# A selective scan in tiles of 4 states x 32 channels, with B and C as broadcast tables

## The chip, the core and the metric

The kernel runs on one core of a Trainium2 chip. The metric is device time in microseconds of one execution, as the median of several runs. Inside the core five engines run side by side, each taking its own instructions in order: TensorE (PE, matrix products), VectorE (DVE), ScalarE (ACT), GpSimd (POOL), and SyncE (SP), whose queue issues most transfers here. The transfers themselves run on 16 DMA engines.

## The reference

The input x is 32 sequences (a batch index b) of 512 tokens with 256 features. A Mamba block, an MLP and a mixture of experts follow one another. What the change touches is the selective scan over 512 inner channels with 16 states each:

```python
xc = silu(conv(xc) + conv_b)
dbc = xc @ x_proj_w.T
dt, Bm, Cm = split(dbc, [16, 32])
dt = softplus(dt @ dt_proj_w.T + dt_proj_b)
A = -exp(A_log)
def step(h, inp):
    dt_t, B_t, C_t, x_t = inp
    dA = exp(dt_t[..., None] * A)
    h = dA * h + (dt_t * x_t)[..., None] * B_t[:, None, :]
    y = einsum('bdn,bn->bd', h, C_t)
    return h, y
y = ys + xc * D_param
y = y * silu(z)
return y @ out_proj_w.T
```

Before it stands a layer norm and the input projection to xc and z. After it come the residual and a layer norm, an MLP with GELU, another layer norm, a router that picks two of eight experts of width 128 beside a shared expert, and a last layer norm. Everything is float32.

## The kernel before

One sequence is one unit of work, and there are 32. For each, `front` normalizes x, transposes it, projects it, does the convolution on DVE (the line of `pin`, L260), and makes dbc, B, C, dt and dt x (`dtx`). dt and dt x are written to scratch in DRAM (`sdt`, `sdx`). B and C are spread over the partitions by two matmuls with the constant `spread` (L291) and copied by ACT to SBUF (`bcr`, tag `bc0` and `bc1`, L293).

The scan needs every channel once for each of its 16 states. A tile has 128 partitions: 16 states times 8 channels (NS = 16, ND = 8), and 512 time steps on the free axis. The 512 channels are 4 blocks j of 128, each of 4 groups q, each of 4 tiles w. A step k takes two of the w (WS = 2) at once, so there are 32 steps for a sequence and 1024 in all. For each step:

- `load` (L336) reads dt and dt x from the scratch with every row repeated for the 16 states: two transfers of 512 KB on SP's queue, into `dtr` (5 buffers) and `u` (8 buffers). The load is written three steps ahead (N_LOAD).
- `times_b` (L356) multiplies u by B in place, on POOL where q is 0, and on DVE for the other three groups. DVE takes B from a PSUM copy (`brep`, one per sequence, L363).
- ACT makes the decay exp(A dt) of each of the two tiles in PSUM (`pda`, two buffers, L420), and DVE runs the recurrence in place in u (L424).
- POOL multiplies u by C (L426).
- When the four w of a group are done, `summed` (L385) adds over the states: four matmuls with the constant `gather` put the sums in four strips of 32 rows of `py` (L388). Each w has its own strip. `skip` (L383) puts D times xc in first.

At the end of a block j DVE multiplies `py` by the gate (L406), and this is xc for the output projection. Since a tile's rows come out in the order w, q, d, the z half of the input projection and the rows of the output projection are stored in that order by the host code.

Beside the scan of sequence b, a generator `fill` runs the `finish` of b - 1: `middle` (projection, MLP), then `front` of b + 1, then `back` (router and experts). The functions yield between pieces, and the loop at the end deals the pieces out over the scan's steps (N_FRONT and N_FINISH are the counts of pieces). The order of instructions in an engine's queue follows this text only roughly: the framework that places tiles moves instructions by its own estimates of when their inputs are ready, as far as the dependencies allow. `later` holds matmuls back: LAG = 1 entry stays in it.

[...] A transposed activation `hT` (MLP) and `x1T` (experts), and `h` and the experts' sum `acc`, have one buffer each.

## Time and profile before

| | |
|---|---|
| median of 3 runs | 5920.9 us (5915.45 to 5924.98) |
| the profiled execution | 5914.54 us |
| its span, first to last instruction | 5912.8 us |
| mean granted TensorE clock | 0.883 |
| moved by DMA | 1184.34 MB, 200 GB/s |

The costliest groups of instructions. Each line has the source line, engine and operation, what is written and read, the shapes and the count; then the busy time, the mean of one in ns, and the idle time of the engine just before it with what ended most of it:

```profile
L426 POOL TENSOR_TENSOR u<-u,bc 128x1024 f32<-128x1024 f32 x1024 | 2411.3, 2358 | 1637.3 <-DVE u L424 961.5
L424 DVE TENSOR_TENSOR_SCAN u<-pda,u 128x512 f32<-128x512 f32 x2048 | 2448.6, 1208 | 193.8 <-ACT pda L420 119.4
L420 ACT ACTIVATE pda<-dtr,a_neg 128x512 f32<-128x512 f32 x2048 | 1401.7, 689 | 1764.1 <-DVE u L424 1666.6
L388 PE MATMUL py<-u,gather 128*32 128x512 f32 x4096 | 1139.3, 682 | 766.1 <-POOL u L426 565.9
L366 DVE TENSOR_TENSOR u<-u,brep 128x1024 f32<-128x1024 f32 x768 | 918.5, 1202 | 200.3 <-DMA u<-sdx 177.6
...
L366 POOL TENSOR_TENSOR u<-u,bc 128x1024 f32<-128x1024 f32 x256 | 603.2, 2357 | 237.7 <-DMA u<-sdx 227.1
```

And the transfers by issue, with the size and the median time from issue to landing in us:

```profile
dtr<-sdt SPq DMA_DIRECT2D x1024, 512.0 KB, 7.3
u<-sdx SPq DMA_DIRECT2D x1024, 512.0 KB, 8.4
sdt<-dt SPq DMA_DIRECT2D x64, 512.0 KB, 2.8
sdx<-dtx SPq DMA_DIRECT2D x64, 512.0 KB, 3.1
x<-in_x_dram SPq DMA_DIRECT2D x32, 512.0 KB, 4.7
out_dram<-acc SPq DMA_DIRECT2D x32, 512.0 KB, 5.8
```

A float32 matmul is two instructions in the profile, so 4096 gather instructions are 2048 matmuls. Busy time of an engine is a sum over the whole span; idle time matters only on an engine that sets the end.

### The profile page before, as it was taken

What the parts mean: (1) busy time and instruction counts of PE and PEld (TensorE: products, weight loads), DVE (VectorE), ACT (ScalarE), POOL (GpSimd) and SP (SyncE); (2) the same over time, 40 slices, a digit from 0 to 9 for tenths busy, and PEclk for the clock granted to TensorE, in tenths of its full rate; (3) what the DMA queues carried; (4) which work ended last, traced back from release to release, by engine and by line L of the source; (5) the groups of instructions that cost most, each with busy time, mean ns of one, the idle gap of its engine ahead of it and who ended that gap; (6) DMA issues with size and microseconds to landing.
All of it is one profiled execution on the core that took longest, in us unless ns stands there. A gap on an engine that the chain in (4) does not pass through costs nothing.

```text
span 5912.8 us, 51778 instructions
## 1 busy us (share of the span) xinstructions
PE 4769.0 (81%) x14464; PEld 2025.0 (34%) x14464; DVE 4936.8 (83%) x7308; ACT 2817.1 (48%) x4224; POOL 3654.8 (62%) x2128
## 2 busy tenths in 40 slices
PE   6688778888788887788887888878888878888787
PEld 1133333333333333333333333333333333333343
DVE  5788888888888888888888888888888888888885
ACT  4445554445544445544455444455444554444542
POOL 3766666656666666666566566666666665666652
PEclk7688889988898898899888898988999888989898
DMA  7978888787887878887878878887878788788871
GB/s 193 239 195 200 211 202 206 201 205 203 207 210 199 210 193 210 199 208 197 209 199 209 203 196 212 201 212 202 206 195 211 194 214 203 198 209 200 210 188 52
DMA packets 367215, 1184.34 MB, mean 200 GB/s; under 512 B 36928, under 2 KB 70848, under 8 KB 366800
## 3 DMA queue, kind: packets, MB, share of 16 engines
q1 hardware_dynamic: 363936, 1175.65, 79.6%
q10 hardware_dynamic: 2992, 5.38, 0.3%
q8 instruction: 117, 1.92, 0.1%
q14 instruction: 170, 1.39, 0.1%
HBM read 1097.00 MB, written 83.89 MB: 200 GB/s over the span
## 4 chain that ended last, share of the span: by engine, by line
PE 29%; DVE 27%; DMA 16%; POOL 14%; issue 8%; ACT 3%; SPq 0%; POOLq 0%; DVEq 0%; ACTq 0%
DMA u<-sdx 16%; DVE u L424 13%; PE py L388 8%; POOL u L426 7%; POOL u L366 4%; DVE acc L574 3%; PE pd L212 3%; PE po L212 3%; DVE u L366 3%; PE pm L205 3%; PE pu L205 2%; PE pdbc L278 2%; PE pg L205 2%; POOL dt L317 2%; DVE the L598 1%
## 5 line engine op out<-in xcount | busy, mean ns | idle before, releaser
L426 POOL TENSOR_TENSOR u<-u,bc 128x1024 f32<-128x1024 f32 x1024 | 2411.3, 2358 | 1637.3 <-DVE u L424 961.5
L424 DVE TENSOR_TENSOR_SCAN u<-pda,u 128x512 f32<-128x512 f32 x2048 | 2448.6, 1208 | 193.8 <-ACT pda L420 119.4
L420 ACT ACTIVATE pda<-dtr,a_neg 128x512 f32<-128x512 f32 x2048 | 1401.7, 689 | 1764.1 <-DVE u L424 1666.6
L388 PE MATMUL py<-u,gather 128*32 128x512 f32 x4096 | 1139.3, 682 | 766.1 <-POOL u L426 565.9
L366 DVE TENSOR_TENSOR u<-u,brep 128x1024 f32<-128x1024 f32 x768 | 918.5, 1202 | 200.3 <-DMA u<-sdx 177.6
L366 POOL TENSOR_TENSOR u<-u,bc 128x1024 f32<-128x1024 f32 x256 | 603.2, 2357 | 237.7 <-DMA u<-sdx 227.1
L205 PE MATMUL pg<-x1T,wg_sb 128*128 128x512 f32 x1152 | 633.0, 656 | 99.1 <-DVE the L598 99.0
L212 PE MATMUL pd<-wd_sb,he 128*128 128x256 f32 x2304 | 647.5, 395 | 43.2 <-DVE acc L574 37.7
L388 PEld LDWEIGHTS py<-u,gather 128*32 128x32 f32 x4096 | 156.4, 114 | 1406.4 <-POOL u L426 880.8
L212 PEld LDWEIGHTS pd<-wd_sb,he 128*128 128x128 f32 x2304 | 410.7, 190 | 501.6 <-DVE acc L574 232.3
L205 PE MATMUL pu<-x1T,wu_sb 128*128 128x512 f32 x1152 | 581.5, 620 | 0.0
L574 DVE SCALAR_TENSOR_TENSOR acc<-pd,cwt,acc 128x256 f32<-128x256 f32 x1024 | 445.8, 470 | 44.6 <-PE pd L212 44.4
L205 PE MATMUL pin<-xnT,in_sb 128*128 128x512 f32 x512 | 310.2, 740 | 81.4 <-DVE xc L272 80.0
L205 PEld LDWEIGHTS pg<-x1T,wg_sb 128*128 128x128 f32 x1152 | 220.5, 205 | 301.8 <-DVE the L598 146.4
L205 PEld LDWEIGHTS pu<-x1T,wu_sb 128*128 128x128 f32 x1152 | 230.6, 200 | 259.5 <-issue 242.4
L260 DVE SCALAR_TENSOR_TENSOR pin<-xpad,half,pin 128x512 f32<-128x512 f32 x384 | 275.0, 744 | 40.9 <-issue 17.1
L205 PE MATMUL pm<-hT,w_sb 128*128 128x512 f32 x512 | 270.2, 676 | 23.2 <-ACT hT L458 23.2
L591 ACT ACTIVATE the<-pg 128x512 f32<-128x512 f32 x288 | 170.3, 591 | 225.3 <-PE pg L205 224.9
L205 PE MATMUL pz<-xnT,in_sb 128*128 128x512 f32 x512 | 263.7, 600 | 0.3 <-DVE the L598 0.3
L212 PE MATMUL po<-out_sb,xc 128*128 128x256 f32 x1024 | 246.9, 394 | 1.6 <-DVE xc L406 1.6
L212 PE MATMUL pm<-w_sb,hid 128*128 128x256 f32 x1024 | 226.2, 379 | 0.0
L212 PEld LDWEIGHTS po<-out_sb,xc 128*128 128x128 f32 x1024 | 194.3, 195 | 89.5 <-DVE u L424 52.0
(112 smaller groups left out, 4911.0 us busy)
## 6 DMA issues: line engine op xcount, KB each, us to landing
dtr<-sdt SPq DMA_DIRECT2D x1024, 512.0 KB, 7.3
u<-sdx SPq DMA_DIRECT2D x1024, 512.0 KB, 8.4
sdt<-dt SPq DMA_DIRECT2D x64, 512.0 KB, 2.8
sdx<-dtx SPq DMA_DIRECT2D x64, 512.0 KB, 3.1
x<-in_x_dram SPq DMA_DIRECT2D x32, 512.0 KB, 4.7
out_dram<-acc SPq DMA_DIRECT2D x32, 512.0 KB, 5.8
wg_sb<-in_w_g_dram ACTq DMA_DIRECT2D x1, 1152.0 KB, 11.7
wu_sb<-in_w_u_dram ACTq DMA_DIRECT2D x1, 1152.0 KB, 6.8
```

The lines of the kernel that those rows point to most:

```text
L205: nc.tensor.matmul(p, w[:, k, cols], src[:, k, :], start=(k == 0), stop=(k == KM - 1))
L212: nc.tensor.matmul(p, part[:, c * P : (c + 1) * P], w[:, j, :], start=(j == 0), stop=(j == len(parts) - 1),)
L260: nc.vector.scalar_tensor_tensor(pa, xp[:, i : i + S], half[:, w0 + i : w0 + i + 1], pa, ALU.mult, ALU.add,)
L278: nc.tensor.matmul(pd[: R + 2 * NS, :], xp_sb[:, j, :], xcs[j], start=(j == 0), stop=(j == NJ - 1),)
L317: nc.gpsimd.tensor_tensor(dt[:, js, :], dt[:, js, :], dtx[:, js, :], ALU.add)
L366: eng.tensor_tensor(u, u, rep.unsqueeze(1).to_broadcast([P, WS, S]), ALU.mult)
L388: nc.tensor.matmul(py[w * n : (w + 1) * n, :], gather[:, q, :], u, start=False, stop=(q == NQ - 1),)
L420: nc.scalar.activation(pda, dtr[:, w, :], AF.Exp, scale=a_neg[:, i : i + 1])
L424: nc.vector.tensor_tensor_scan(uw, pda, uw, 0.0, ALU.mult, ALU.add)
L426: nc.gpsimd.tensor_tensor(u, u, bcr[1].unsqueeze(1).to_broadcast([P, WS, S]), ALU.mult)
L574: nc.vector.scalar_tensor_tensor(a, p, cw[:, c, e : e + 1], a, ALU.mult, ALU.add)
L591: nc.scalar.activation(th, pg, AF.Tanh, scale=0.5)
```

## The change

A tile now holds 4 states of 32 channels (NP = 4, ND = 32), with the 512 time steps as before. A block j of 128 channels is 4 groups c of 32, and the 16 states are 4 groups of 4, taken two at a time (GS = 2), so a step is (b, j, c, g) with g 0 or 1, and there are again 32 steps of two tiles for a sequence.

- `load` brings dt and dt x of a group c once, as tiles of 256 KB (`dtr`, `dxr`, three buffers each), with each row repeated for 4 states. Both steps of the group, four tiles, use them. The load is written two groups ahead.
- B and C differ over the states of a tile, and no longer only by partition copies made on the chip: `front` writes the 32 rows of B and C to scratch (`rows`), and `table` reads them back, repeated over the 32 channels, as four tables of 512 KB for a sequence (two halves g of each; three buffers for B and three for C). The spread matmuls and their copies go.
- `times_b` multiplies dt x by B into a new tile u. Where DVE does it (c from 1 to 3), dt x is first copied by ACT to the PSUM bank that `brep` had (`dx`, one buffer), once for each group c.
- `summed` has one 128 x 32 `gather`; it runs for a pair of groups c - 1 and c at the same g, so its four matmuls go to two strips of `py`, each twice. `later` counts in steps, LAG = 2.
- A block's rows are now in natural order, and the host code no longer permutes the projections.
- `acc` is `h` itself, and `hT` and `x1T` share a buffer (`mT`). `front` has one piece fewer.

```diff
@@ -26,16 +26,19 @@
 EPS = 1e-5
 
 
-ND = P // NS
-W = 4
-NQ = P // (W * ND)
+
+NP = 4
+NG = NS // NP
+ND = P // NP
+NC4 = P // ND
+GS = 2
 
 
...
@@ -116,32 +119,13 @@
 
 
 
-
-    spread = const.tile([R + 2 * NS, 2, P], F32, name="spread")
-    for a in range(2):
-        n0 = R + a * NS
-        nc.vector.tensor_copy(
-            spread[:, a, :].rearrange("p (n d) -> p n d", d=ND),
-            ident[: R + 2 * NS, n0 : n0 + NS].unsqueeze(2).to_broadcast(
-                [R + 2 * NS, NS, ND]
-            ),
-        )
-    gather = const.tile([P, NQ, NQ * ND], F32, name="gather")
-    nc.gpsimd.memset(gather, 0.0)
-    for q in range(NQ):
-        nc.vector.tensor_reduce(
-            gather[:, q, q * ND : (q + 1) * ND],
-            ident.rearrange("p (n d) -> p d n", d=ND),
-            AX.X,
-            ALU.add,
-        )
+    gather = const.tile([P, ND], F32, name="gather")
+    nc.vector.tensor_reduce(
+        gather, ident.rearrange("p (d n) -> p d n", n=NP), AX.X, ALU.add
+    )
     skip = const.tile([P, NJ, P], F32, name="skip")
     for j in range(NJ):
-        nc.vector.tensor_scalar_mul(
-            skip[:, j, :].rearrange("p (w q d) -> p w q d", w=W, q=NQ),
-            ident.rearrange("p (q d w) -> p w q d", w=W, q=NQ),
-            col("dp", j),
-        )
+        nc.vector.tensor_scalar_mul(skip[:, j, :], ident, col("dp", j))
 
     out_sb = const.tile([P, NJ, DM], F32, name="out_sb")
     w1_sb = const.tile([P, KM, 2 * DM], F32, name="w1_sb")
...
@@ -285,14 +269,8 @@
         yield
         dbc = work.tile([R + 2 * NS, S], F32, tag="dbc", name=f"dbc_{b}", bufs=1)
         nc.scalar.copy(dbc, pd[: R + 2 * NS, :])
-        bcr = []
-        for a in range(2):
-            pb = ps.tile([P, S], F32, tag="tk", name=f"pbc_{b}_{a}")
-            nc.tensor.matmul(pb, spread[:, a, :], dbc, start=True, stop=True)
-            t = work.tile([P, S], F32, tag=f"bc{a}", name=f"bc{a}_{b}")
-            nc.scalar.copy(t, pb)
-            bcr.append(t)
-        yield
+        rows = scr.tile([2, NS, S], F32, tag="rows", name=f"rows_{b}")
+        nc.sync.dma_start(rows.rearrange("a n t -> (a n) t"), dbc[R : R + 2 * NS, :])
 
 
         dt = work.tile([P, NJ, S], F32, tag="dt", name=f"dt_{b}", bufs=1)
...
-
-
-
+        got[b] = (xt, xnT, xcs, rows, sdt, sdx)
+
+
+
+
+    NH = NG // GS
     steps = [
-        (b, j, q, w)
+        (b, j, c, g)
         for b in range(NB)
         for j in range(NJ)
-        for q in range(NQ)
-        for w in range(0, W, WS)
+        for c in range(NC4)
+        for g in range(NH)
     ]
-    dtrs, us, breps = {}, {}, {}
+    per = NJ * NC4 * NH
+    dtrs, dxrs, dxps, us, bcs = {}, {}, {}, {}, {}
 
     def load(k):
-        b, j, q, w = steps[k]
+
+        b, j, c, _ = steps[k]
         _, _, _, _, sdt, sdx = fronts[b]
-        for tag, src, into, bufs in (
-            ("dtr", sdt, dtrs, DT_BUFS),
-            ("u", sdx, us, U_BUFS),
-        ):
-            t = work.tile([P, WS, S], F32, tag=tag, name=f"{tag}_{b}_{j}_{q}_{w}", bufs=bufs)
-            rows = src[j, q * W * ND : (q + 1) * W * ND, :]
+        for tag, src, into in (("dtr", sdt, dtrs), ("dxr", sdx, dxrs)):
+            t = work.tile([P, S], F32, tag=tag, name=f"{tag}_{b}_{j}_{c}", bufs=DT_BUFS)
             nc.sync.dma_start(
-                t.rearrange("p w t -> p (w t)"),
-                rows.rearrange("(d w) t -> d w t", w=W)[:, w : w + WS, :]
+                t,
+                src[j, c * ND : (c + 1) * ND, :].unsqueeze(1).to_broadcast([ND, NP, S]),
+            )
+            into[k // NH] = t
+
+    def table(a, b, g):
+
+        if (a, b, g) not in bcs:
+            t = work.tile([P, GS, S], F32, tag=f"bc{a}", name=f"bc{a}_{b}_{g}", bufs=NH + 1)
+            n0 = g * GS * NP
+            nc.sync.dma_start(
+                t.rearrange("p g t -> p (g t)"),
+                fronts[b][3][a, n0 : n0 + GS * NP, :]
+                .rearrange("(n g) t -> n (g t)", g=GS)
                 .unsqueeze(0)
-                .to_broadcast([NS, ND, WS, S]),
-            )
-            into[k] = t
+                .to_broadcast([ND, NP, GS * S]),
+            )
+            bcs[a, b, g] = t
+        return bcs[a, b, g]
 
     def by_pool(k):
         return steps[k][2] == 0
 
     def times_b(k):
-        b = steps[k][0]
+        b, j, c, g = steps[k]
+        kc = k // NH
         if by_pool(k):
-            eng, rep = nc.gpsimd, fronts[b][3][0]
+            eng, dx = nc.gpsimd, dxrs[kc]
         else:
-            if b not in breps:
-                breps[b] = ps.tile([P, S], F32, tag="brep", name=f"brep_{b}", bufs=1)
-                nc.scalar.copy(breps[b], fronts[b][3][0])
-            eng, rep = nc.vector, breps[b]
-        u = us[k]
-        eng.tensor_tensor(u, u, rep.unsqueeze(1).to_broadcast([P, WS, S]), ALU.mult)
+            if kc not in dxps:
+                dxps[kc] = ps.tile([P, S], F32, tag="dx", name=f"dx_{b}_{j}_{c}", bufs=1)
+                nc.scalar.copy(dxps[kc], dxrs[kc])
+            eng, dx = nc.vector, dxps[kc]
+        u = work.tile([P, GS, S], F32, tag="u", name=f"u_{b}_{j}_{c}_{g}", bufs=U_BUFS)
+        eng.tensor_tensor(
+            u, dx.unsqueeze(1).to_broadcast([P, GS, S]), table(0, b, g), ALU.mult
+        )
+        us[k] = u
 
     def ahead(k):
 
-        if k + N_LOAD < len(steps):
-            load(k + N_LOAD)
+        if k % NH == 0 and k + N_LOAD * NH < len(steps):
+            load(k + N_LOAD * NH)
         if k + 1 < len(steps) and by_pool(k + 1):
             times_b(k + 1)
         if k < len(steps) and not by_pool(k):
             times_b(k)
 
     def scan(b):
-        xt, xnT, ys, bcr, _, _ = fronts[b]
+        xt, xnT, ys, _, _, _ = fronts[b]
+
 
         later = []
 
         def skipped(j, py):
             nc.tensor.matmul(py, skip[:, j, :], ys[j], start=True, stop=False)
 
-        def summed(q, py, tiles):
-            n = NQ * ND
-            for w, u in enumerate(tiles):
-                nc.tensor.matmul(
-                    py[w * n : (w + 1) * n, :],
-                    gather[:, q, :],
-                    u,
-                    start=False,
-                    stop=(q == NQ - 1),
-                )
+        def summed(py, c, g, pair):
+
+            for i in range(GS):
+                for dc, u in enumerate(pair):
+                    r = (c + dc) * ND
+                    nc.tensor.matmul(
+                        py[r : r + ND, :],
+                        gather,
+                        u[:, i, :],
+                        start=False,
+                        stop=(g == NH - 1 and i == GS - 1),
+                    )
 
         def gate(j):
 
...
@@ -405,36 +402,32 @@
         def gated(j, py, th):
             nc.vector.scalar_tensor_tensor(ys[j], py, 0.5, th, ALU.mult, ALU.mult)
 
-        per = len(steps) // NB
-        tiles = []
         for k in range(b * per, (b + 1) * per):
-            _, j, q, w0 = steps[k]
-            u, dtr = us.pop(k), dtrs.pop(k)
-            if q == 0 and w0 == 0:
+            _, j, c, g = steps[k]
+            u, dtr = us[k], dtrs[k // NH]
+            if c == 0 and g == 0:
                 py = ps.tile([P, S], F32, tag="py", name=f"py_{b}_{j}", bufs=1)
-                later.append(partial(skipped, j, py))
+                later.append((k + LAG, partial(skipped, j, py)))
             ahead(k + 1)
-            for w in range(WS):
-                pda = ps.tile([P, S], F32, tag="pda", name=f"pda_{b}_{j}_{q}_{w0 + w}")
-                i = (j * NQ + q) * W + w0 + w
-                nc.scalar.activation(
-                    pda, dtr[:, w, :], AF.Exp, scale=a_neg[:, i : i + 1]
-                )
-                uw = u[:, w, :]
-                nc.vector.tensor_tensor_scan(uw, pda, uw, 0.0, ALU.mult, ALU.add)
-                tiles.append(uw)
-            nc.gpsimd.tensor_tensor(
-                u, u, bcr[1].unsqueeze(1).to_broadcast([P, WS, S]), ALU.mult
-            )
-            if len(tiles) == W:
-                later.append(partial(summed, q, py, tiles))
-                tiles = []
-                if q == NQ - 1:
-                    later.append(partial(gated, j, py, gate(j)))
-                while len(later) > LAG:
-                    later.pop(0)()
-            yield
-        for f in later:
+            if k == (b + 1) * per - 2 * NC4 and b + 1 < NB:
+                table(0, b + 1, 0)
+                table(1, b + 1, 0)
+            for i in range(GS):
+                pda = ps.tile([P, S], F32, tag="pda", name=f"pda_{b}_{j}_{c}_{g}_{i}")
+                a = (j * NC4 + c) * NG + g * GS + i
+                nc.scalar.activation(pda, dtr, AF.Exp, scale=a_neg[:, a : a + 1])
+                ui = u[:, i, :]
+                nc.vector.tensor_tensor_scan(ui, pda, ui, 0.0, ALU.mult, ALU.add)
+            nc.gpsimd.tensor_tensor(u, u, table(1, b, g), ALU.mult)
+            if c % 2 == 1:
+                pair = (us.pop(k - NH), us.pop(k))
+                later.append((k + LAG, partial(summed, py, c - 1, g, pair)))
+                if c == NC4 - 1 and g == NH - 1:
+                    later.append((k + LAG, partial(gated, j, py, gate(j))))
+            while later and later[0][0] <= k:
+                later.pop(0)[1]()
+            yield
+        for _, f in later:
             f()
 
...
@@ -447,7 +440,7 @@
             nc.vector.tensor_tensor(h[:, c, :], xt[:, c, :], po[:, :DM], ALU.add)
         mr, rs = layernorm(h, f"b{b}")
         yield
-        hT = work.tile([P, KM, S], F32, tag="hT", name=f"hT_{b}", bufs=1)
+        hT = work.tile([P, KM, S], F32, tag="mT", name=f"hT_{b}", bufs=1)
 
         def get(c):
...
@@ -533,8 +526,8 @@
     def back(b, h):
         mr, rs = layernorm(h, f"c{b}")
         yield
-        acc = work.tile([P, NC, DM], F32, tag="acc", name=f"acc_{b}", bufs=1)
-        x1T = work.tile([P, KM, S], F32, tag="x1T", name=f"x1T_{b}", bufs=1)
+        acc = h
+        x1T = work.tile([P, KM, S], F32, tag="mT", name=f"x1T_{b}", bufs=1)
 
         def get(c):
             normalize(acc[:, c, :], h[:, c, :], mr, rs, c)
...
     run(front(0, fronts))
     load_late_weights()
-    for k in range(N_LOAD):
-        load(k)
+    for i in range(N_LOAD):
+        load(i * NH)
+    table(1, 0, 0)
     times_b(0)
     ahead(0)
     fill, n_fill = (front(1, fronts), 2 * N_FRONT) if NB > 1 else (iter(()), 0)
     for b in range(NB):
...
 
-LAG = 1
-WS = 2
-N_LOAD = 3
-N_FRONT = 30
-N_FINISH = 88
-DT_BUFS = 5
+LAG = 2
+N_LOAD = 2
+N_FRONT = 29
+N_FINISH = 87
+DT_BUFS = 3
 U_BUFS = 8
...
     def states(v):
 
-        v = v.reshape(NJ, NQ, ND, W, NS)
-        return v.transpose(4, 2, 0, 1, 3).reshape(P, -1)
-
-
-    o = _np.arange(DI).reshape(NJ, NQ, ND, W).transpose(0, 3, 1, 2).reshape(-1)
-    in_w = a["attn_in_proj_w"]
-    in_w = _np.concatenate([in_w[:DI], in_w[DI:][o]], axis=0)
+        v = v.reshape(NJ, NC4, ND, NG // GS, NP, GS)
+        return v.transpose(2, 4, 0, 1, 3, 5).reshape(P, -1)
...
         ("x", a["attn_x"]),
         ("vecs", vecs),
-        ("in_w", in_w.T),
+        ("in_w", a["attn_in_proj_w"].T),
         ("xp_w", a["attn_x_proj_w"].T),
         ("dt_w", a["attn_dt_proj_w"].T),
-        ("out_w", a["attn_out_proj_w"].T[o]),
+        ("out_w", a["attn_out_proj_w"].T),
         ("m_w1", a["attn_mlp_w1"].T),
```

## What the change is predicted to do

> **What bounds the kernel now.** I read the busy shares first, then the slices in time, the chain of waits, the waits of each engine, and last one batch cut into its stages.
>
> ```profile
> PE 4769.0 (81%) x14464; PEld 2025.0 (34%) x14464; DVE 4936.8 (83%) x7308; ACT 2817.1 (48%) x4224; POOL 3654.8 (62%) x2128
> ...
> DMA  7978888787887878887878878887878788788871
> ...
> q1 hardware_dynamic: 363936, 1175.65, 79.6%
> ...
> PE 29%; DVE 27%; DMA 16%; POOL 14%; issue 8%; ACT 3%; SPq 0%; POOLq 0%; DVEq 0%; ACTq 0%
> DMA u<-sdx 16%; DVE u L424 13%; PE py L388 8%; POOL u L426 7%; POOL u L366 4%; DVE acc L574 3%; PE pd L212 3%; PE po L212 3%; DVE u L366 3%; PE pm L205 3%; PE pu L205 2%; PE pdbc L278 2%; PE pg L205 2%; POOL dt L317 2%; DVE the L598 1%
> ```
>
> No engine is full: VectorE (DVE) works 4936.8 of 5912.8 us, so it idles 976, and that is all a change that leaves its work alone can win. The DMA engines are busy to 7 or 8 tenths in every slice, and the largest single piece of the last chain is a transfer, the load of u (16%, some 946 us). What of it costs DVE time is in the waits:
>
> ```profile
> DVE u L366 <- DMA u<-sdx: 177.6, 79, 4.2
> DVE acc L572 <- PE pd L212: 168.0, 62, 6.7
> DVE u L424 <- ACT pda L420: 119.4, 112, 5.1
> DVE h L485 <- PE pm L212: 102.6, 35, 16.8
> ...
> DVE st_a L175 <- DMA x<-in_x_dram: 51.4, 29, 5.4
> DVE acc L574 <- PE pd L212: 44.4, 98, 1.3
> ...
> DVE u L424 <- POOL u L366: 22.0, 7, 5.8
> ...
> POOL u L366 <- DMA u<-sdx: 227.1, 135, 6.9
> POOL u L426 <- DMA u<-sdx: 168.6, 34, 7.1
> ...
> ACT pda L420 <- DMA dtr<-sdt: 87.7, 40, 2.7
> ```
>
> DVE waits directly for DMA (177.6 + 51.4), and behind ACT and GpSimd (POOL) that wait for it. A second family, 315 us (168.0 + 102.6 + 44.4), is DVE waiting for matmuls; TensorE (PE) runs in order, and its gather matmuls wait for POOL. One batch by stages (from 2947 us: MLP, next front's convolution, its dt part, experts):
>
> ```profile
> 2947.00:2985.00 38.00, 28.24 (x90) 13.82 (x89) 28.81 (x44) 21.13 (x31) 27.64 (x19) 0.87 0.81 207
> 2985.00:3030.00 45.00, 30.87 (x88) 8.75 (x89) 39.42 (x50) 22.61 (x37) 28.77 (x20) 0.81 0.93 222
> 3030.00:3060.00 30.00, 26.18 (x63) 9.58 (x62) 22.69 (x31) 20.00 (x29) 18.97 (x9) 0.72 0.63 176
> 3060.00:3130.00 70.00, 64.74 (x217) 30.93 (x216) 63.39 (x107) 24.33 (x39) 38.75 (x20) 1.00 0.79 204
> ```
>
> The columns after the length are busy time of PE, weight loads, DVE, ACT, POOL, then PE's clock, DMA share and GB/s. DVE idles 9.2, 5.6, 7.3 and 6.6 us, 28.7 in 183. In the expert stage PE is 92% busy at full clock: there PE is a second bound.
>
> **What the Trainium skill says.** "Perfetto Trace Analysis", Identifying the Most-Contended Engine: occupancy is a fair measure for the vector engines, matmul busy time is not. So DVE's 83% is read as a floor and PE's 81% is not; the trace agrees, since the same gather group takes 1.05 or 1.92 us with the clock. "DMA: Bandwidth & Descriptors", Specifications: line rate needs pieces of at least 512 B. The new loads have 2 KB rows instead of 4 KB; the trace has 2 KB rows in the writes of dt (512 KB landed in 2.8 us), so I see no penalty beyond a bounded one. "TensorEngine Tiling (Array Packing)", Key Properties: different tiles of the array run in parallel. The trace agrees (the gather of four tiles, eight instructions, takes 1.06 us; that of one, two instructions, 1.05). "GPSIMD Engine Reference", Specifications: its SBUF interface is shared with DVE when DVE has two SBUF inputs. That is avoided before (brep in PSUM) and after (dx in PSUM); DVE's multiplication stays one SBUF and one PSUM input, so I keep its 1202 ns.
>
> **Part by part.**
>
> *Loads.* Gone: 2048 loads of 512 KB (dtr, u), 1073.7 MB. New: 1024 of 256 KB (dtr, dxr), 268.4 MB, 128 tables of 512 KB, 67.1 MB, 32 small writes of rows, 2 MB. Of 1184 MB some 448 are left: DMA share 79.6 x 448 / 1184 = 30% at the same rate, 50% at worst with the smaller rows. Either way the queue is open. Loads are asked for two channel groups ahead (four steps, some 22 us at 5.77 us per step = 5912.8 / 1024), against 7.3 and 8.4 us to landing now. So direct waits go: 177.6 all; of 51.4 for x some 40 (the landing itself stays); of the 119.4 for the exponentials some 60, since ACT's wait for dtr is 87.7; of the 22.0 for POOL's product 20. Together 298. Bounds: 178 (u alone) and 339 (177.6 + 51.4 + 87.7 + 22.0).
>
> *What POOL's lateness costs.* POOL waits 227.1 + 168.6 = 396 us for u. PE waits 566 us for POOL's products, and 200 for a POOL queue held up elsewhere. I give PE's share 396 / 766 = 0.52 of the 315 us that DVE waits for matmuls: 163. Below it is 0, if POOL is then late for another reason; above, 315.
>
> *Multiplication by B.* 768 on DVE at 1202 ns and 256 on POOL at 2357, as before; the output is now a new tile. It needs no transfer into u, so a u buffer is taken at the product, not a DMA earlier. Tiles of a pair wait two steps longer for their gather, and LAG is 2: the eight buffers are held about as long as before without the transfer. Zero.
>
> *Copies of dx.* 12 per batch, 384 x 592 ns (row of brep's copy) = 227 us on ACT, less 64 copies of bc (37.1) and 32 of brep (18.9): +171, ACT goes from 48 to 51%. ACT idles 1667 us waiting for the scan, which hides them. But there is one bank: the copy must wait for DVE's last product with the old dx, and DVE's next product waits for the copy. In the changed program's order two to eight DVE instructions (2.4 us and more) stand between. Only at the batch end do four normalizations, which now wait 3.9 us for POOL's mr_d once a batch, stand between two copies; behind the waiting product on DVE are scans, for which POOL waits. I take 0.1 us a copy: 38. Bounds 0 and 0.8 us a copy (307).
>
> *Gather matmuls.* Still 2048 (4096 instructions), but a group of four now falls on two column strips (c and c+1), each twice in turn. Two can run side by side, where eight instructions of four tiles take 1.06 us now. I went through both instruction orders, counting each unbroken run as 0.85 us per layer and 0.2 for its start: 26.9 us a batch before (the trace has 1139.3 / 32 = 35.6, with cold clocks and broken runs), 36.1 after. So +9.2 us a batch, 2.6 in the expert stage, 6.6 elsewhere. The two spread matmuls save 66.3 in all, not on the path. The 2.6 count in full (PE 92% busy): 83. Of the 6.6 a fifth, PE being 69 to 87% busy there: 42. Together 125. Bounds: 0 and 294.
>
> *Tables.* Four per batch. Those of the second half are asked for when first used, so POOL stands once or twice a batch for a transfer of some 5 us; behind it on POOL are C products, with PE two steps behind. On SP's queue the C table waits for POOL's last use of the old one, with the output write and a load for two groups ahead behind it. I take 1 us a batch on DVE's path: 30; bounds 0 and 100.
>
> *acc in h, hT and x1T in one buffer, LAG, constants.* The next h waits for the output write (5.8 us to landing); the last normalizations stand in ACT's order ahead of exponentials for six scans and a product, over 8 us of DVE work, that come before it. Zero, at most 3 us a batch (93) without that cover.
>
> Sum: 5912.8 - 298 - 163 + 38 + 125 + 30 = 5646 as a span. The profiled run took 5914.5 with 1.7 around its span, and the median of the runs is 6.4 above it, so 5654; I say **5655 us**. DVE would then idle some 710 us instead of 976. What is late next: PE in the expert stage, the normalization chain over POOL and ACT after each batch's scan, and DVE itself.
>
> **Rivals.**
> 1. *DVE's floor comes nearer* (15%). DMA held back more than its own waits show: direct 339, all 163 of POOL's, gather and copies hidden: 5921 - 502 = 5419, reaching up to 5500. For it: 16% of the chain is the u load. Against: the expert stage has few DMA waits and a full PE.
> 2. *PE takes the place of DMA* (18%). All 9.2 us a batch land on the path (294), POOL's part does not return: 5921 - 298 + 294 - 66 = 5851 with the spread matmuls saved; between 5770 and 5909. For it: PE at 92% with experts. Against: in the other three stages PE idles 28 us of 113 (9.8 + 14.1 + 3.8), at clocks of 0.72 to 0.87.
> 3. *The single dx bank makes it slower* (12%). Every change of channel group is a chain DVE, ACT, DVE. With t us of stall on each of 384 copies, gather 125 and tables 30, it loses as soon as 384 t + 155 passes 461, t = 0.8 us. ACT is in order, and an ACT instruction waiting for PE or POOL (225 us for pg, 126 for mr_b) ahead of a copy would give that. At t = 1.5: 5921 + 576 + 155 - 461 = 6191. Against: the slack in the order above.
>
> **How the numbers follow.** Forecast 55% (5500 to 5770), rivals 15, 18 and 12. Measurements tell 0.2% (12 us) from no change. Of the second rival 3 points lie within that, and 1 of the third: same 0.04. Slower 0.11, faster 0.85. The range leaves out about half of rival 1 and most of rival 3: 5440 to 5870.
>
> **What would show it.** DMA share 30 to 50%. The waits of DVE and POOL for u by DMA gone, and no wait for the table or dxr above 60 us in their place. DVE busy within 1% of 4937. Gather busy up by 200 to 350 us. DVE's wait for the dx copy under 60 us; above 300 rival 3 is right. A DVE wait for pd and pm above 350 us with PE over 88% busy means rival 2. The prediction fails if DVE's idle time stays above 900 us or falls below 500.

## The result, and the profile after

| | before | after |
|---|---|---|
| median, 4 runs each on one chip | 5922.9 us | 5846.0 us (5845.5 to 5850.2) |
| ratio, 95% interval | | 0.9873 (0.9856 to 0.9890) |
| span of the profiled run | 5912.8 us | 5843.9 us |
| DVE busy, idle | 4936.8, 976.0 | 4950.2, 893.7 |
| moved by DMA | 1184 MB | 448 MB |

The change makes the kernel faster by 1.3%, 77 us, where 266 were forecast. Of all executions in this document one, of the later run onecopy_fix, took 7420.2 us at a mean granted TensorE clock of 0.602 instead of 0.917, and it is left out of that run's figures.

Busy times, the main DMA queue and the last chain, from the page of after:

```profile
PE 4875.3 (83%) x14336; PEld 2073.3 (35%) x14336; DVE 4950.2 (85%) x7303; ACT 2965.3 (51%) x4512; POOL 3649.2 (62%) x2127
...
q1 hardware_dynamic: 236448, 439.49, 22.6%
...
DVE 42%; PE 36%; POOL 9%; ACT 7%; issue 4%; DMA 0%; ACTq 0%; DVEq 0%; POOLq 0%
DVE u L420 21%; PE py L385 11%; DVE u L357 6%; PE pg L189 6%; PE pd L196 6%; POOL u L421 5%; PE pu L189 4%; DVE pin L244 4%; DVE h L567 2%; PE pm L189 2%; PE pm L196 2%; ACT pda L418 2%; POOL dt L295 2%; PE pz L189 1%; POOL dtx L297 1%
```

DMA is gone from the chain (16% before) and idle for three quarters of the time. Still DVE idles 894 us. What it waits for now, by total us, number of waits and the longest:

```profile
DVE m L501 <- PE pg L543: 198.2, 32, 10.4
DVE u L420 <- ACT pda L418: 117.3, 96, 2.5
DVE xc L403 <- PE py L385: 113.2, 66, 8.6
DVE the L591 <- ACT the L584: 99.9, 68, 2.1
DVE u L357 <- ACT dx L354: 78.1, 31, 2.5
DVE h L478 <- PE pm L196: 74.7, 35, 17.5
DVE h L565 <- PE pd L196: 61.5, 63, 1.3
DVE h L567 <- PE pd L196: 51.3, 100, 0.8
...
DVE st_a L159 <- DMA x<-in_x_dram: 7.8, 3, 5.4
```

The 177.6 us for u are gone, those for x fell from 51.4 to 7.8, and those for pd and pm from 315 to 187.5. Against that, four waits grew by 424 us: the router's maximum for pg from 16.4 to 198.2, the expert's tanh from 12.2 to 99.9, the gate for py from 36.5 to 113.2, and the copy of dx, which is new, 78.1. Only the last belongs to an edit directly. In before these lines read:

```profile
DVE xc L406 <- PE py L388: 36.5, 36, 9.5
...
DVE m L508 <- PE pg L550: 16.4, 3, 10.3
...
DVE the L598 <- ACT the L591: 12.2, 10, 5.6
```

Where the largest arises is seen in the timeline of one batch (start, duration, and in brackets the idle time before with its releaser):

```profile
2983.03 3.63 PE L385 MATMUL py<-u,gather 128*32 128x512 f32 x8 [0.74 <-POOL u L421]
2983.29 1.21 DVE L357 TENSOR_TENSOR u<-dx,bc 128x1024 f32<-128x1024 f32 x1
2983.33 1.91 ACT L291 ACTIVATE dt<-dt 128x2048 f32<-128x2048 f32 x1
2985.14 0.57 ACT L537 COPY x1T<-tp_c 128x512 f32<-128x512 f32 x1
...
2988.63 1.62 PE L543 MATMUL pg<-gt_sb,x1T 128*128 128x8 f32 x14
...
2990.29 0.19 DVE L501 TENSOR_REDUCE m<-pg 128x4 f32<-128x32 f32 x1 [5.79 <-PE pg L543]
```

DVE's reduction L501 stands in its queue ahead of two scans. It waits 5.79 us for router products that stand on PE behind eight gather instructions of 3.63 us, and whose input x1T stands on ACT behind the logarithm of dt. No transfer and no full engine holds this up; it is where the instructions stand. The clock has a part in it: from 2983.00 to 2987.00 us TensorE was granted 0.55 of full speed on the mean, and the eight gather instructions took 3.63 us, where the same eight take 1.91 us at a granted clock of 1.00 (after_sched3, below). They took 3.5 us or more ahead of the router in 30 of the 32 batches, so some 1.7 us of each such wait is put down to the clock here. This is an estimate from these two durations, and no run tests it.

### The profile page after: what moved, and what is told of

Its sections match the earlier page's. It is cut to its first block, busy times and chain, and to the rows that moved or that the text cites. A ratio compares the mean times of both kernels' runs of the same rounds, so it can differ in the third digit from the quotient of the medians.

```text
span 5843.9 us, 47922 instructions
## 1 busy us (share of the span) xinstructions
PE 4875.3 (83%) x14336; PEld 2073.3 (35%) x14336; DVE 4950.2 (85%) x7303; ACT 2965.3 (51%) x4512; POOL 3649.2 (62%) x2127
## 3 DMA queue, kind: packets, MB, share of 16 engines
q1 hardware_dynamic: 236448, 439.49, 22.6%
## 4 chain that ended last, share of the span: by engine, by line
DVE 42%; PE 36%; POOL 9%; ACT 7%; issue 4%; DMA 0%; ACTq 0%; DVEq 0%; POOLq 0%
DVE u L420 21%; PE py L385 11%; DVE u L357 6%; PE pg L189 6%; PE pd L196 6%; POOL u L421 5%; PE pu L189 4%; DVE pin L244 4%; DVE h L567 2%; PE pm L189 2%; PE pm L196 2%; ACT pda L418 2%; POOL dt L295 2%; PE pz L189 1%; POOL dtx L297 1%
## 5 line engine op out<-in xcount | busy, mean ns | idle before, releaser
L421 POOL TENSOR_TENSOR u<-u,bc 128x1024 f32<-128x1024 f32 x1024 | 2410.5, 2356 | 1778.4 <-DVE u L420 1691.1
L420 DVE TENSOR_TENSOR_SCAN u<-pda,u 128x512 f32<-128x512 f32 x2048 | 2439.5, 1211 | 121.4 <-ACT pda L418 117.3
L385 PE MATMUL py<-u,gather 128*32 128x512 f32 x4096 | 1389.1, 664 | 442.0 <-POOL u L421 393.9
L357 DVE TENSOR_TENSOR u<-dx,bc 128x1024 f32<-128x1024 f32 x768 | 923.6, 1210 | 83.2 <-ACT dx L354 78.1
L385 PEld LDWEIGHTS py<-u,gather 128*32 128x32 f32 x4096 | 238.5, 115 | 1249.6 <-POOL u L421 606.5
L357 POOL TENSOR_TENSOR u<-dxr,bc 128x1024 f32<-128x1024 f32 x256 | 602.4, 2353 | 4.8 <-PE py L385 2.8
L196 PEld LDWEIGHTS pd<-wd_sb,he 128*128 128x128 f32 x2304 | 421.0, 189 | 403.9 <-DVE h L567 168.0
L567 DVE SCALAR_TENSOR_TENSOR h<-pd,cwt,h 128x256 f32<-128x256 f32 x1024 | 450.0, 480 | 55.6 <-PE pd L196 51.3
L196 PE MATMUL po<-out_sb,xc 128*128 128x256 f32 x1024 | 303.0, 452 | 53.8 <-DVE h L440 28.6
L189 PE MATMUL pin<-xnT,in_sb 128*128 128x512 f32 x512 | 252.0, 625 | 52.9 <-DVE xc L256 49.8
L262 PE MATMUL pdbc<-xc,xp_sb 128*48 128x512 f32 x256 | 175.0, 846 | 131.9 <-DVE xc L256 131.8
L591 DVE SCALAR_TENSOR_TENSOR the<-the,pg 128x512 f32<-128x512 f32 x288 | 195.8, 680 | 99.9 <-ACT the L584 99.9
L189 PE MATMUL pm<-hT,w_sb 128*128 128x512 f32 x512 | 239.3, 611 | 43.2 <-ACT hT L451 22.6
```

Source lines behind the costliest of these rows:

```text
L189: nc.tensor.matmul(p, w[:, k, cols], src[:, k, :], start=(k == 0), stop=(k == KM - 1))
L196: nc.tensor.matmul(p, part[:, c * P : (c + 1) * P], w[:, j, :], start=(j == 0), stop=(j == len(parts) - 1),)
L262: nc.tensor.matmul(pd[: R + 2 * NS, :], xp_sb[:, j, :], xcs[j], start=(j == 0), stop=(j == NJ - 1),)
L357: eng.tensor_tensor(u, dx.unsqueeze(1).to_broadcast([P, GS, S]), table(0, b, g), ALU.mult)
L385: nc.tensor.matmul(py[r : r + ND, :], gather, u[:, i, :], start=False, stop=(g == NH - 1 and i == GS - 1),)
L420: nc.vector.tensor_tensor_scan(ui, pda, ui, 0.0, ALU.mult, ALU.add)
```

## The experiments

Ratios are to the kernel before on the same chip. The measured medians, with the runs of before from 5911.6 to 5929.6:

| run | us | ratio (95%) |
|---|---|---|
| wide | 5890.2 | 0.9948 (0.9933 to 0.9962) |
| b_narrow | 5835.4 | 0.9858 (0.9841 to 0.9876) |
| b_quarter | 5789.3 | 0.9777 (0.9762 to 0.9791) |
| b_quarter_narrow | 5698.9 | 0.9626 (0.9611 to 0.9640) |
| before_ordn | 5842.0 | 0.9883 (0.9853 to 0.9914) |
| wide_fix | 5796.9 | 0.9812 (0.9783 to 0.9841) |
| onecopy_fix | 5847.1 | 0.9871 (0.9849 to 0.9893) |
| b_quarter_fix | 5910.5 | 1.0001 (0.9988 to 1.0014) |
| b_half_fix | 5752.0 | 0.9710 (0.9691 to 0.9730) |
| after_more | 6734.7 | 1.1376 (1.1347 to 1.1405) |
| after_order | 5808.2 | 0.9832 (0.9798 to 0.9866) |
| after_sched | 5456.8 | 0.9214 (0.9196 to 0.9232) |
| before_sched | 5785.8 | 0.9764 (0.9744 to 0.9783) |
| b_half_sched | 5768.1 | 0.9739 (0.9719 to 0.9759) |
| wide_sched | 5462.7 | 0.9225 (0.9209 to 0.9240) |
| after_sched2 | 5545.1 | 0.9364 (0.9348 to 0.9380) |
| after_sched3 | 5418.0 | 0.9140 (0.9125 to 0.9155) |
| before_sched3 | 5528.8 | 0.9328 (0.9313 to 0.9343) |

### One part alone, the order left to the framework

**wide**: after with the gathers in four strips.

```diff
-                    r = (c + dc) * ND
+                    r = (2 * i + dc) * ND
```

> The changed kernel with the four gather matmuls of a pair sent to four strips of py instead of two (strip 2i + dc), so that all four can run side by side. The sums then land in wrong rows: this is a price, not a version. Theory A (the narrower gather on PE took the gain): gather busy time falls from 1389 to 1000 us or less and the time by 100 us or more, to 5746 or less. Theory B (the order around the router, with dt on ACT and POOL, sets the batch's length): gather busy falls the same, the time by less than 40 us, to 5806 or more.

**b_narrow**: before with the gathers in two strips at a time.

```diff
-                    py[w * n : (w + 1) * n, :],
+                    py[(q % 2 * 2 + w % 2) * n : (q % 2 * 2 + w % 2 + 1) * n, :],
```

> The kernel before with the four gather matmuls of a group on two strips of py, as in the changed kernel (the two strips change with q). The sums land in wrong rows. Theory A: gather busy rises from 1139 to about 1350 us, and the time by 50 us or more, to 5970 or more, part of it hidden behind the DMA waits. Theory B: the time moves by less than 20 us.

**b_quarter**: before with one load of dt and dt x for four steps, and a new u. **b_quarter_narrow** has both edits.

```diff
-            into[k] = t
+            for i in range(4):
+                into[k + i] = t
...
-        if k + N_LOAD < len(steps):
-            load(k + N_LOAD)
+        if k % 4 == 0 and k + 4 < len(steps):
+            load(k + 4)
```

> The kernel before with its loads alone cut: dt and dt x are loaded once for two groups q (two tiles of 512 KB for four steps), and all four steps use them, so that three steps of four compute with another step's rows; the product with B goes into a new u tile. The gather stays on four strips, B stays in one PSUM copy. DMA share falls from 80% to about 25%. Theory A: what DMA was worth without the narrower gather comes out in full: 250 us or more off, to 5670 or less. Theory B: the same router chain stands in the way: 60 to 130 us off, 5790 to 5860.

> The two edits to the kernel before together: loads cut to a quarter, and the gather on two strips. It has the changed kernel's DMA share and gather width without its tables, its dx copies and its other buffers. Theory A: near the changed kernel, 5800 to 5880, and 100 us or more slower than with the loads cut alone. Theory B: within 40 us of the kernel with the loads cut alone.

The theories A and B, as the expectations word them, both fell with the first two runs. With four strips the gather's busy time fell from 1389 to 1082 us, and the kernel was 44 us slower than after. With two strips the kernel before was 86 us faster, at about the same busy time of the gather (1127 for 1139). So this edit did not make the gather dearer, as it was meant to, and puts no price on the two strips. The instruction order differs in both: the framework's estimates change with a strip, and it moves instructions on every engine. The cut of the transfers gave 132 us alone (5921.0 - 5789.3) and 137 beside b_narrow. Hence theory C: the order sets the time, and each edit acts twice, by its work and by the order that it brings about. To separate the two, all later kernels are held to a given order. A dependency that needs no semaphore is laid from each instruction to the next of its engine; `order` is a list of positions:

```python
for x in order[engine]:
    if last is not None:
        add_manual_dep(instructions[x], last, NoSync)
    last = instructions[x].name
```

### One part alone, the order held

**before_ordn**: before, in the order of b_narrow.

> The kernel before, with nothing left out or changed in its work, held on PE, DVE, ACT, POOL and SP to the instruction order that the run b_narrow had. If that run was faster by its order alone (theory C): about 5835, 75 to 95 us less than the kernel before. If its two strips were what made it faster: 5900 to 5940, the time of the kernel before.

It is 1.2% faster with the same work; b_narrow was 1.4%. So the order alone is worth some 70 us, nearly the whole measured effect of the change. Two more pairs below have the same edit with and without a held order: wide and wide_fix differ by 93 us (5890.2 and 5796.9), b_quarter and b_quarter_fix by 121 us (5789.3 and 5910.5).

**wide_fix**: wide, in the order of after.

> The kernel after with its gathers in four strips, as in the run wide, but now every engine is held to the instruction order of the kernel after by ordering dependencies, so that only the strips differ. The rows i = 0 and i = 1 of a pair of groups are put in different strips instead of being added, so the sums of the scan stand in wrong rows; the work on the other engines is the same. Gather busy should fall from 1389 to about 1080 us, as in wide. Theory A (the gather's PE time is on the path): 120 to 200 us less than the kernel after, 5650 to 5730. Theory C (order and waits set the time, the width of the gather does not): within 40 us of the kernel after, 5805 to 5860.

Against after, the medians differ by 49 us and the ratios by 0.6% (36 us). The gather's busy time fell by 359 us (1389.1 to 1029.9). The busy time of PE as a whole fell by 240 us (4875.3 to 4635.1), as other products took longer; the mean granted clock was 0.877 instead of 0.917. So a tenth to a seventh of the gather's saving reaches the end, between the two expectations.

**onecopy_fix**: dt x is copied to PSUM once for a block.

```diff
         else:
+            kc -= c - 1
             if kc not in dxps:
```

> The kernel after with dt x copied to PSUM once for each block of 128 channels instead of three times, so that two of three copies go and DVE multiplies the wrong channels' dt x in groups 2 and 3; all engines held to the order of the kernel after, without the 256 copies. DVE's wait for the copy (78 us, two thirds of it 52) and ACT's 149 us of copies go. My term for the copies was 38 us, so 25 for two thirds: 5800 to 5830. If other waits take it over: 5835 to 5855. If the copies hold the exponentials back more than their own wait shows: below 5780.

No change: 5847.1 for 5846.0. DVE's waits, in the trace of onecopy_fix:

```profile
DVE u L421 <- ACT pda L419: 198.8, 97, 4.1
DVE m L502 <- PE pg L544: 198.4, 32, 10.5
```

The wait for the copy (78.1 us) is gone from the list, and the wait for the exponential of the scan behind it has grown by 81.5 (117.3 to 198.8). Every other line is as in after to within a us. This is how a wait is replaced: as far as these sums show, DVE reaches the next instruction earlier and waits there for the same moment.

**b_quarter_fix**: b_quarter, with PE, DVE and ACT in the order of before.

> The kernel before with its loads of dt and dt x cut to a quarter, as in b_quarter (four steps share one load of a group, so three of four steps scan the wrong channels), held on PE, DVE and ACT to the instruction order of the kernel before; POOL and SP are free. So only the transfers change. My forecast for this part of the change: direct waits 298 and POOL's lateness 163, hence 5460. If POOL's lateness does not go back: 5620 to 5650. If most of what the transfers held up is taken over by other waits: 5760 to 5850. b_quarter without the fixed order had 5789.

**b_half_fix**: half of each load, so that all five engines can be held.

```diff
-                t.rearrange("p w t -> p (w t)"),
-                rows.rearrange("(d w) t -> d w t", w=W)[:, w : w + WS, :]
+                t[:, 0, :],
+                rows.rearrange("(d w) t -> d w t", w=W)[:, w, :]
...
-        eng.tensor_tensor(u, u, rep.unsqueeze(1).to_broadcast([P, WS, S]), ALU.mult)
+        eng.tensor_tensor(u, fronts[b][3][1].unsqueeze(1).to_broadcast([P, WS, S]), rep.unsqueeze(1).to_broadcast([P, WS, S]), ALU.mult)
...
-                    pda, dtr[:, w, :], AF.Exp, scale=a_neg[:, i : i + 1]
+                    pda, dtr[:, 0, :], AF.Exp, scale=a_neg[:, i : i + 1]
```

> The kernel before with both loads of a step cut from two tiles to one, 256 KB instead of 512; both exponentials of a step read the first tile's dt, and u is made as B times C into the loaded tile, so that it still waits for the load; all five engines held to the order of the kernel before. If the transfers' waits are covered by that order, as in b_quarter_fix where POOL was free: 5880 to 5925. If b_quarter_fix hid a gain by POOL's other order: 5600 to 5800.

b_quarter_fix gave nothing, b_half_fix 166 us (5917.9 - 5752.0). In b_quarter_fix DVE's direct waits for u (177.6 us) are gone and those for x fell from 51.4 to 20.0, but these four lines grew by 250 us together, from 102.6, 168.0, 119.4 and 11.4 in before:

```profile
DVE h L486 <- PE pm L212: 210.8, 35, 16.8
DVE acc L573 <- PE pd L212: 207.9, 62, 6.6
DVE u L425 <- ACT pda L421: 151.4, 129, 2.9
DVE pin L260 <- ACT pin L252: 81.1, 27, 9.6
```

The run had another order on POOL, and took its u buffers at the product: there POOL waits 97.7 us for gathers (6.8 in before). So its zero is not that of the transfers alone; which of the two cost the difference was not isolated. In b_half_fix every instruction stands in its place, and half of each load is left. The product with B reads another tile, at the same price (1206 ns for 1202 on DVE). Its DVE waits:

```profile
DVE h L485 <- PE pm L212: 200.0, 35, 16.8
DVE acc L572 <- PE pd L212: 136.1, 47, 5.8
DVE u L424 <- ACT pda L420: 125.2, 116, 4.1
...
DVE acc L574 <- PE pd L212: 41.1, 77, 1.2
...
DVE u L366 <- DMA u<-sdx: 30.1, 18, 3.0
DVE st_a L175 <- DMA x<-in_x_dram: 30.0, 27, 6.2
```

DVE's own waits for DMA fell by 169 us (147.5 for u, 21.4 for x), and the time by 166. The waits for pd and pm rose, from 315 to 377, though POOL's wait for u had gone from 227 to 26 (groups of POOL); that for the exponential rose from 119 to 125. The two near figures, 169 and 166, are not the same microseconds: other waits fell too, such as the idle time before a scan in which DVE waited for nothing that the profile shows (37.8 to 0) and the wait for POOL's product with C (12.8 to 0). What is shown is the sum: of the 461 us that I had counted, 166 came back for half of the loads.

**after_more**: after with the old volume on SP's queue.

```diff
+        for src in (sdt, sdx):
+            more = scr.tile([ND, 3 * NP, S], F32, tag="more", name=f"more_{b}_{j}_{c}")
+            nc.sync.dma_start(more, src[j, c * ND : (c + 1) * ND, :]
+                .unsqueeze(1).to_broadcast([ND, 3 * NP, S]))
```

> The kernel after with all of its work, and with each pair of loads followed on SP by two transfers of 768 KB of the same rows from scratch to scratch that nothing reads, so that a group moves 2 MB through the queue as in the kernel before; PE, DVE, ACT and POOL held to the order of the kernel after. If the transfers were what the kernel before waited for (my forecast): 6000 to 6250, waits by DMA back in front of ACT, DVE and POOL. If their waits are covered by other waits of the order (theory C): 5840 to 5900.

6734.7, slower than any expectation. The added transfers also write to DRAM, and loads and tables stand behind them: ACT waits 517 us for dxr, POOL 401 for it and 334 for a table, which lands after 10.8 us instead of 4.5. So it is not the mirror of the cut that I meant. It suggests that after has little lead over its loads, and needs the light queue that it has.

### The order itself

**after_order**: three places of each batch moved, in after's own order. As lists of lines, of batch 15, before the edit and after it:

```
PE   385 x4, 543, expert 8, 543 x7   ->  543 x8, 385 x4, expert 8
PE   385 x2, expert 0, pd            ->  expert 0, pd, 385 x2
DVE  501, 502, 420, 505, 420         ->  420, 501, 502, 420, 505
```

Here xN counts matmuls, 543 is a router product, 385 a gather, 420 a scan; expert 8 is the shared expert and expert 0 the first routed one.

> The kernel after with all of its work, held to its own order except for three places in each batch's experts and router: the eight router products stand ahead of the gathers that the scheduler had put before them on PE; the two gathers that stood before the first routed expert's products stand behind its first down product; on DVE the router's maximum and difference stand one scan later, and its sum one scan later. Theory C (the router's head-of-line waits of DVE, 198 us for pg and part of 100 us for the tanh, are on the path): 100 to 200 us less than the kernel after, 5650 to 5750. If the time lost there only moves to the next wait: within 40 us of it, 5805 to 5860.

By the medians 38 us faster than after, by the ratios 24, and the intervals of the two ratios overlap a little. The router's wait fell from 198.2 us to 10.2, but those for the exponentials and the tanh grew from 117.3 and 99.9 us:

```profile
DVE u L420 <- ACT pda L418: 235.1, 126, 3.7
DVE the L591 <- ACT the L584: 169.3, 69, 5.4
```

As in onecopy_fix most of it moves on, so these single waits taken out by hand gave little.

**after_sched** and **before_sched**: all five queues made anew, for each kernel from its own durations.

> The kernel after with all of its work, each engine held to a new order of its instructions. The order was made by placing one instruction after another on the engine that is free first, by the mean durations of the trace of after, the longest remaining chain and the order of the text deciding between several that are ready. Theory C (the order sets the time): 5150 to 5400; DVE's busy time of 4950 and some 200 at both ends of the run are the floor, and an estimate from the same durations ends at 5150 to 5310. If an engine or a resource that the durations do not show is the limit: within 100 us of after_order, 5700 to 5850.

> The kernel before with all of its work, each engine held to an order made in the same manner from its own trace. The difference to after_sched is what the change is worth once the order of neither is the limit. If the transfers then bind (DMA at 80% of a span of 5913 would be 90% of one of 5250): 5500 to 5800, well above after_sched. If they are hidden by a good order as well: 5230 to 5450, within 100 us of after_sched.

after_sched is 389 us faster than after, five times what the change gave, with the same instructions, though slower than I expected. before_sched gained only 132. That lies within my range for transfers that bind, but b_half_sched, below, contradicts this reading.

**b_half_sched** is the edit of b_half_fix in the order of before_sched, **wide_sched** that of wide in the order of after_sched.

> The same edit with all five engines held to the order of before_sched (5786). If the transfers are what keeps before_sched 329 us above after_sched: 5450 to 5600. If it is the order itself (the eight buffers of u that a load takes three steps ahead): 5740 to 5790.

> The kernel after with its gathers in four strips as in wide (sums in wrong rows), held to the order of after_sched (5457, PE 93% busy). The gather's busy time should fall by 300 us or more. My term for the gather was 125 us at the order that I assumed; at the order of after it measured 35 to 50. If PE is the limit of after_sched: 5250 to 5370. If DVE is: 5400 to 5455.

Neither moves its kernel by more than 0.3%: 5768.1 for 5785.8, and 5462.7 for 5456.8. So the 329 us between the two were not the transfers. wide_sched is a weak test of the gather: its busy time fell by only 140 us (1620.6 to 1480.2), not by the 300 or more that I expected.

**after_sched2**: placed anew with the longer gathers of after_sched.

> The kernel after with all of its work, in an order made like that of after_sched, but from the durations that the trace of after_sched shows (a gather instruction 0.396 us of busy time instead of 0.339). If durations are what the order was wrong in: 5370 to 5440. If its limit is elsewhere: 5440 to 5480.

88 us slower than after_sched and outside both expectations, and PE was 96% busy, the gather alone with 1903.9 us. Its trace shows why (start, duration; the instruction count is last):

```profile
2990.93 1.05 PE L385 MATMUL py<-u,gather 128*32 128x512 f32 x2
...
2993.82 1.05 PE L385 MATMUL py<-u,gather 128*32 128x512 f32 x4
```

One matmul (two instructions) takes as long as two that go to different strips. The placement had given each gather a price of its own and let it stand anywhere; standing singly, it pays double. In this run 1402 of the 2048 gather matmuls stand alone.

**after_sched3** and **before_sched3**: four gather matmuls stay together.

> The kernel after with all of its work, in an order made like that of after_sched with one more rule: the four gather matmuls of a call stand one behind the other on PE. In after_sched2, where they stood singly between other products, the gather took 0.465 us of busy time for an instruction, in after_sched 0.396, in after 0.339. If gathers share the array only when they follow one another, the figure goes back to about 0.34 and PE's busy time to about 4880: 5330 to 5440. If the order of after_sched is as good without it: 5440 to 5500.

> The kernel before with all of its work, in an order made by the same rules as after_sched3. In before_sched the gather took 0.377 us for an instruction instead of 0.278, and PE 423 us more. If that kept before_sched at 5786: 5480 to 5650, and the change is worth some 150 to 250 us in good orders. If something else keeps it there: 5720 to 5800.

The busy times of after_sched3:

```profile
PE 4614.7 (85%) x14336; PEld 2010.9 (37%) x14336; DVE 4972.1 (92%) x7303; ACT 2961.3 (55%) x4512; POOL 3655.6 (67%) x2127
```

and a gather in its timeline, now four matmuls in 1.91 us:

```profile
2988.41 1.91 PE L385 MATMUL py<-u,gather 128*32 128x512 f32 x8
```

The gather's busy time fell to 1067.0 us, 0.260 for an instruction and less than the 0.34 that I expected. after_sched3 is the best version, 8.6% under the kernel before and 7.3% under after. before_sched3 is 257 us faster than before_sched by the rule. There the transfers show again, in the DMA queue, the chain and the waits of DVE and POOL:

```profile
q1 hardware_dynamic: 363936, 1175.65, 84.5%
...
DVE 45%; PE 24%; DMA 11%; POOL 9%; ACT 6%; issue 5%; SPq 0%; POOLq 0%; ACTq 0%; DVEq 0%
DVE u L424 20%; DMA u<-sdx 9%; DVE u L366 7%; DVE acc L574 4%; POOL u L366 4%; PE pm L205 4%; POOL u L426 4%; PE pdt L304 3%; DVE pin L260 3%; PE pin L205 3%; PE py L388 3%; PE pd L212 3%; ACT pda L420 2%; DVE he L599 2%; PE py L383 2%
```

```profile
DVE u L424 <- POOL u L366: 158.4, 79, 4.5
...
POOL u L366 <- DMA u<-sdx: 223.5, 60, 9.8
```

No run cuts the loads at this order, so what they cost there is not shown.

Placed by the same rules, the two kernels differ by 111 us (2.0%), under the 150 to 250 that I expected. This is the difference of one placement of each; it includes what the placement makes of each structure, and another rule can give another figure, as the 329 us of the first rule show.

## Why the prediction was wrong in its size

The sign was right, and 5846 lies within the range. The forecast of 5655 was 191 us too low. (Its terms add up to 5645 as a span, not 5646, and four steps are 23 us, not 22; neither matters.)

- *Transfers, -298 and -163.* This is the step that failed: the 461 us that the waits for transfers were to give back. At the order of before, half of each load taken away gave 166 us (b_half_fix; 647 MB are left, in after 448). With three of four loads gone the kernel gained 132 and 137 us in the framework's own orders, and nothing in b_quarter_fix. Of the 298, DVE's direct waits for u and x fell by 169 us in b_half_fix and by 209 in b_quarter_fix. The 60 us of the exponentials' wait and the 20 of POOL's product did not come back (125.2 for 119.4, 20.8 for 22.0 in b_half_fix). Of the 163 of POOL's lateness nothing is to be seen: with POOL's waits gone, DVE waited 62 us more for pd and pm. I had added up waits as if each came back in full, and taken a share of PE's waits for a share of DVE's.
- *Gather, +125.* At the order of after 359 us of the gather's time were worth 36 to 49 (wide_fix), so by the same share the 250 that the change added are worth some 25 to 34, an estimate from these figures. In wide_sched 140 us of it were worth nothing. The busy time rose inside the 200 to 350 that I named, so the work was right and its share on the path too large.
- *Copies, +38.* The wait was there and larger (78.1 us against my limit of 60), but two thirds of the copies taken out gave nothing (onecopy_fix).
- *Multiplication by B, 0.* The product kept its price on DVE, 1210 ns for 1202. No run gives it two inputs from SBUF, so the sharing with POOL that the prediction cites was not tested.
- *Tables, +30,* were not measured alone. The longest total wait for a table is 3.7 us, on POOL, far below the 60 that I named.
- *The order, 0.* A term that I did not have. I read the changed order for stalls, but took it as a backdrop, while it is itself worth 70 us at equal work (before_ordn) and 428 in after (5846.0 to 5418.0).

With 43 for the gather, nothing for the copies and my own 30 for the tables, the sum is -166 + 43 + 0 + 30 = -93, against -77. The agreement is luck as far as is known: the 166 are for half of the loads, the 43 for more gather time than the change added, the 30 were not measured, and the framework's order moves the time by as much as the rest.

The rivals: the second had 5851, but by another mechanism. Its sign was a wait for pd and pm above 350 us with PE over 88% busy; they are 187.5 and 83%. The chain has PE at 36% for 29% before and DVE at 42% for 27%, so more of it runs over PE, but not over an engine out of time. The third did not come. The first had 5419 to 5500; after_sched and after_sched3 end there, but by their order, which is not its mechanism. DVE's idle time, 894 us, stays just under the 900 at which I called the prediction failed.

## What to carry to other kernels

A sum of waits is no forecast of a gain, not even of waits directly in front of the engine that sets the end. Of 78 us taken away there nothing came back in onecopy_fix, of 188 for the router 24 to 38 us in after_order, of 209 for transfers nothing in b_quarter_fix; only in b_half_fix was the gain as large as the direct waits removed, 166 for 169. Take one wait away in a run, at a held order, and see where it goes. Where a framework orders the instructions, an edit changes the order too, and that can outweigh the edit: compare at a held order before a cause is named. And look at the order itself as something to tune: here it gave 428 us, and the edit 77.

## What the hardware showed that I had not expected

- A matmul's price depends on its neighbours. One gather alone took 1.05 us, two in different strips together 1.05, so the same 4096 instructions cost from 1067.0 (after_sched3) to 1903.9 us (after_sched2) of PE time. The clock is not the reason, since after_sched2 had the higher mean, 0.964 for 0.937. "TensorEngine Tiling (Array Packing)", Key Properties, of the Trainium skill has tiles of the array run in parallel; the traces agree, and add that the order decides whether they do.
- The clock is a second part of a matmul's price. In before a single gather took 1.05 us in places and 1.92 in others; in after eight gather instructions took 3.63 us where the granted clock was 0.55, against 1.91 at 1.00 in after_sched3. (In the prediction I read the first two durations as bearing out what I cite there on matmul busy time; what they show is the clock's part.)
- A transfer's own time is not fixed. The queue's packets took 64 us of one DMA engine's time for a MB before (79.6% of 16 engines for 5912.8 us, over 1175.65 MB), and 56 in b_quarter, whose loads have the same form (22.5% of 5784.5 us, over 370.25 MB). In after it was 48. The lighter queue is not the whole reason: in after_more it was 48 too, at 55.8% of 6725.5 us over 1244.87 MB. The form of the transfers differs there as well, and the two were not separated. I had scaled the share with the volume, to 30%; it was 22.6%.
- PE's share of busy time says little of its limit: 93% in after_sched and 91% in wide_sched at the same time, and 85% in the faster after_sched3.
